# Two graph-transformer layers on one core: the 20-token tile moved to the last block of each layer and spread over four column tiles of the array

## The chip, the cores and the metric

One core of one Trainium2 chip. The time is device microseconds from the first to the last instruction's work of one execution; the number to predict is the median of the runs of the changed kernel. All matrices are float32.

## The reference, cut to what matters

There are 2708 tokens of 512 features and a sparse symmetric adjacency with the diagonal set (about 9 neighbours of a token, never more than 23 counted with itself). Each of two layers does:

```python
q, k, v = h @ Wq.T + bq, h @ Wk.T + bk, h @ Wv.T + bv      # 8 heads of 64
attn    = softmax(where(mask, q.k / 8, -1e9))               # over the neighbours
h1 = layer_norm(h + (attn @ v) @ Wo.T + bo)
h2 = layer_norm(h1 + relu(h1 @ W1.T + b1) @ W2.T + b2)      # 512 -> 2048 -> 512
```

The second layer takes the first one's `h2` as its `h`.

## The kernel before, in words

`by_edges` never builds the 2708 x 2708 scores. It first lists each token's neighbours, sorts the tokens by how many they have, and cuts the sorted order into 22 tiles, numbered 0 (most neighbours) to 21. 2708 is 21 times 128 plus 20, so tile 21 has only 20 tokens, and these have the fewest neighbours. `CAPS` gives the neighbour slots of each tile: 22 for tile 0, 6 for tile 19, 5 for tile 20, 3 for tile 21. (`by_rows` is a dense fallback behind a branch that these inputs do not take.)

Attention of a tile works slot by slot on VectorE (DVE), ScalarE (ACT) and GpSimd (POOL). For each slot POOL gathers one key-and-value row for every token (line 982). The slots go in chunks of up to two: DVE multiplies by the queries (line 1019) and sums by head (line 1025), ACT takes the exponential (line 1038), ACT and DVE scale the values (lines 1045 and 1051), and DVE adds them up (line 1058). When a tile's slots are through, DVE makes the sums and reciprocals (lines 1066 to 1081) and ACT writes the divided context `cx` (line 1089). A tile of 20 tokens costs as much per slot as one of 128, since the cost goes with the row length.

TensorE (PE) does the dense part. `project` (line 569) is four accumulating products, one per 128 features, with the tokens as the stationary operand and 512 weight columns moving: it makes k, v, q and the output projection o. `feed_forward` takes a block of two tiles side by side: in each of 16 steps f it makes a 128-feature slice of the hidden layer (`pf`, line 1312: the weights are stationary, the block's tokens move, so 148 or 256 columns), ACT applies relu (`ft`, line 1320), and three steps later (`LAG`) each of the block's two tiles gets its second product, 512 columns moving, into its own accumulator `a` (line 1300). Then DVE adds the residual (line 1332) and normalises (lines 1128 to 1138, with one power on POOL at line 1134).

Eleven blocks make a layer. Before, the order is (21, 20), (19, 18), (8, 9), (7, 10), (6, 11), (0, 17), (1, 16), (2, 15), (3, 14), (4, 13), (5, 12). Attention follows the same order and runs ahead of PE by credits: `advance` lets some chunks be issued per step, `through(k)` issues everything until block k's contexts exist. Late in block k (step 10 or 11) the contexts of block k+1 are transposed (`tp<-ident,cx`, line 1144), projected with Wo, normalised, and in the last step transposed again (`tp<-ident,h`) as the next block's input. Beside the next block's steps the first layer makes the second layer's k and v of the finished block (`keys_values`, lines 1362 to 1376).

The first block of a layer is special, since there is no block before it to hide its attention. In layer 0 it runs beside `first_queries` (22 projections, line 909 takes them out of PSUM); the first tiles' own queries are computed from gathered rows by `own_query` (line 955), so that their attention need not wait for the stored queries. In layer 1 it runs beside 16 of the layer's query projections (line 1242), and can start only when the last block's k and v are in memory.

The order on PE, ACT and the SP queue is written out by hand; DVE and POOL are ordered by a planner, except where they too are set by hand.

Of the kernel before, what the change touches and what calls it, by code (L numbers as in the profile page):

```python
# [19 lines left out]
DM = 512  # L20
# [11 lines left out]
SAFE = 60.0  # L32
LIST = 24
SEG = 247

CAPS = (22, 14, 13, 12, 12, 11, 11, 10, 10, 9, 9, 9, 9, 8, 8, 8, 7, 7, 7, 6, 5, 3)
SLOTS = 2
# [7 lines left out]
QT = 6  # L45
OWN = 13
EARLY = 3
FIRST = 4
PACE = (0.62, 0.72)


# [420 lines left out]
def by_edges(ctx: ExitStack, tc: tile.TileContext, x, xT, adj, layers, out, good):  # L472
# [92 lines left out]
    def project(xs, r, wm, name, other=False):  # L565

        o = (ps_f if other else ps).tile([P, DM], F32, tag="f" if other else "g", name=name)
        for c in range(NC):
            nc.tensor.matmul(o[:r], xs(c), wm[:, c, :], start=(c == 0), stop=(c == NC - 1))  # L569
        return o  # L570

    def finish(steps):
        for _ in steps:
# [7 lines left out]
    def size(g):  # L581
        return min(P, N - g * P)
# [231 lines left out]
    def first(w, meanwhile):  # L814

        xg = []

        def load():
            i = len(xg)
            b = i % XBS * XB  # L820
            bw = min(XB, N - b)
            t = wts.tile([P, NC, XB], F32, tag=f"w1_{5 + i % 3}", name="xg")
            xg.append(t)
            step = bw if i else P
            for a in range(0, bw, step):
# [24 lines left out]
        wv = matrix(w, "Wv", "wv")  # L850
        pa = tc.tile_pool(name="pa", bufs=2)
        lists, counted, ranked, listed = lists_of(pa.__enter__())
        done, before = 0, None
        for t in range(NT):
            r = size(t)
            xs = tokens(t, 0)
            kv = wts.tile([P, 2 * DM], F32, tag=f"w2_{5 + t % 3}", name="kvs")
            k = project(xs, r, wk, "k")
            if t == 0:
                finish(turning)  # L860
            nc.vector.tensor_tensor(kv[:r, :DM], k[:r], bk[:r], ALU.add)
            v = project(xs, r, wv, "v", other=True)
            nc.scalar.copy(kv[:r, DM:], v[:r])
            if before:
                nc.scalar.dma_start(**before)
            before = dict(out=kv_d[0][t * P : t * P + r, :], in_=kv[:r])
            if t == 0:
                finish(load())
            while done < min(NT, 1 + LEAD * t):
                lists(done)  # L870
                done += 1
                if done == NT:
                    counts = counted()
            meanwhile(t)
            if t == QT:
                wq = matrix(w, "Wq", "wq")
                turning = turned_row(cols[1], "bq", DK**-0.5)
                bq = next(turning)
                finish(turning)
        nc.scalar.dma_start(**before)  # L880
        return bq, wq, counts, ranked, listed, pa, tokens

    def first_queries(bq, wq, counts, ranked, listed, pa, tokens, meanwhile):
# [14 lines left out]
        for t in range(NT):  # L898
# [7 lines left out]
            if t % 2 == 0:  # L906
# [2 lines left out]
            nc.vector.scalar_tensor_tensor(  # L909
                qs[:r, t % 2], q[:r], DK**-0.5, bq[:r], ALU.mult, ALU.add  # L910
            )
            if t == OWN - 1:
# [38 lines left out]
    def own_query(g, zT, to, bq, wq):  # L951

        r = size(g)
        q = project(lambda c: zT[:, c, :r], r, wq, "q")
        nc.vector.scalar_tensor_tensor(to[:r], q[:r], DK**-0.5, bq[:r], ALU.mult, ALU.add)

    def checked():

# [194 lines left out]
    class Layer:  # L1153
# [83 lines left out]
        def query(self, g, zT):  # L1237

            r = size(g)
            q = project(lambda c: zT[:, c, :r], r, self.wq, "q")  # L1240
            qs = dn.tile([P, DM], F32, tag="row", name="qs", bufs=3)
            nc.vector.scalar_tensor_tensor(
                qs[:r], q[:r], DK**-0.5, self.bq[:r], ALU.mult, ALU.add
            )
            self.kept()
            self.due = (g, qs)

# [7 lines left out]
        def attended(self, block, got):  # L1255
# [11 lines left out]
            for g, r, cT, xb in cTs:  # L1267
                o = project(lambda c: cT[:, c, :r], r, self.wo, "o")
                h = dn.tile([P, DM], F32, tag="h", name="h", bufs=4)
                nc.vector.tensor_tensor(h[:r], o[:r], xb[:r], ALU.add)  # L1270
                if self.n == 0:
                    nc.vector.tensor_tensor(h[:r], h[:r], self.bo[:r], ALU.add)
                norm(h, r, self.g1, self.e1b2)
# [13 lines left out]
        def feed_forward(self, block, hs, hT):  # L1287
# [5 lines left out]
            def second(f, only=None):  # L1293
                c0 = 0
                for g, a in zip(block, accs):
                    r = size(g)
                    if only not in (None, g):
                        c0 += r
                        continue
                    nc.tensor.matmul(  # L1300
# [3 lines left out]
                        start=(f == 0),  # L1304
                        stop=(f == NFC - 1),
                    )
                    c0 += r

            for f in range(NFC):
# [11 lines left out]
                fts.append(ft)  # L1321
                if f >= LAG:
                    second(f - LAG)
                yield None
            for g in block:
                for f in range(NFC - LAG, NFC):
                    second(f, g)
            zs = []
            for g, a, h in zip(block, accs, hs):
                r = size(g)  # L1330
                z = h
                nc.vector.tensor_tensor(z[:r], a[:r], h[:r], ALU.add)  # L1332
                norm(z, r, self.g2, self.e2)
                if self.n == NL - 1:
                    nc.gpsimd.indirect_dma_start(
# [10 lines left out]
        def keys_values(self, block, zs):  # L1346
# [12 lines left out]
            for i, (g, z, zT) in enumerate(zip(block, zs, zTs)):  # L1359
                r = size(g)  # L1360
                kv = kvs[:, i, :]
                k = project(lambda c: zT[:, c, :r], r, self.kv[0], "k")
                nc.vector.tensor_tensor(kv[:r, :DM], k[:r], self.bk[:r], ALU.add)
                v = project(lambda c: zT[:, c, :r], r, self.kv[1], "v")
                nc.scalar.copy(kv[:r, DM:], v[:r])
                nc.sync.dma_start(out=zT_d[n][g], in_=zT)
                nc.sync.dma_start(out=xb_d[n][g * P : g * P + r, :], in_=z[:r])
                yield
# [293 lines left out]
```

## Time and profile before

| what | value |
|---|---|
| three runs, median (lowest to highest) | 1954.73 us (1953.54 to 1954.83) |
| the profiled execution, span | 1950.7 us |
| PE busy in it | 1892.6 us (97%) |
| DVE, ACT, POOL busy | 1300.1, 933.4, 797.9 us |
| mean granted TensorE clock | 0.992 |

The profiled span is 4.0 us below the median of the three runs. In the rows, a float32 product of TensorE is two records, each with its own load of the stationary operand; `128*20` behind an operation means 128 rows and 20 columns of the array in use, `128*128` all of it. A record's duration [...]overlaps the next one, so the pace of a row of products is read from start to start.

### The profile page before, as it was taken

The numbers are of one execution on the slowest core, as the hardware profiler recorded it, in microseconds if no ns is written. First come the engines' busy times: TensorE is split into PE (matmuls) and PEld (weight loads), VectorE is DVE, ScalarE is ACT, GpSimd is POOL, SyncE is SP. The second block draws the span as 40 slices with busy tenths as digits, with TensorE's granted clock in tenths as the row PEclk, the third lists the DMA queues.
The fourth block names the chain that finished last, engine by engine and source line by source line (L and its number), as shares of the span: only waits on it lengthen the run. The fifth ranks groups of instructions, "written<-read, shape, count | busy, mean of one in ns | idle before, by whom it ended". The sixth has DMA issues, their size and how long they took to land.

```text
span 1950.7 us, 20853 instructions
## 1 busy us (share of the span) xinstructions
PE 1892.6 (97%) x6162; PEld 1100.7 (56%) x6162; DVE 1300.1 (67%) x2142; ACT 933.4 (48%) x3219; POOL 797.9 (41%) x710
## 2 busy tenths in 40 slices
PE   9999988999999898999999999999999999999997
PEld 4444433565656555566565643556666666666664
DVE  5884576685957859577552116898597989877421
ACT  4660254464555655446441112665457765755410
POOL 3114535453644636445210004554255756554110
PEclk9999998999999999999999999999999999999999
DMA  9998766554745746455320548756465757563000
GB/s 330 355 307 296 265 211 219 177 193 137 235 153 173 235 146 231 146 177 190 110 90 22 194 152 315 253 207 207 137 236 169 253 188 265 184 202 127 11 11 13
DMA packets 131487, 366.92 MB, mean 188 GB/s; under 512 B 16669, under 2 KB 36989, under 8 KB 128655
## 3 DMA queue, kind: packets, MB, share of 16 engines
q0 software_dynamic: 69120, 246.35, 38.0%
q1 hardware_dynamic: 53332, 99.66, 14.9%
q10 hardware_dynamic: 8910, 19.48, 2.6%
q8 instruction: 50, 0.82, 0.2%
q14 instruction: 75, 0.61, 0.1%
HBM read 314.62 MB, written 50.83 MB: 187 GB/s over the span
## 4 chain that ended last, share of the span: by engine, by line
PE 54%; issue 3%; DVE 2%; POOL 1%; DMA 1%; ACT 1%; POOLq 0%; SPq 0%; DVEq 0%
PE a L1300 21%; PE pf L1312 21%; PE o L569 5%; PE q L569 2%; PE k L569 2%; PE v L569 2%; PE tp L1144 1%; POOL kv L982 1%; DVE kv L1019 0%; DVE sc L1025 0%; DMA zT<-zT_d 0%; DMA kv<-kv_d,idx 0%; ACT hT L1149 0%; ACT kv L1045 0%; DMA kv_d<-kvs,ident_i 0%
## 5 line engine op out<-in xcount | busy, mean ns | idle before, releaser
L982 POOL DMA_INDIRECT kv<-kv_d,idx x420 | 540.6, 1287 | 459.8 <-DVE acc L1058 265.3
L1300 PE MATMUL a<-w,ft 128*128 128x512 f32 (+1 forms) x1408 | 663.7, 597 | 3.2 <-ACT ft L1320 3.2
L1312 PE MATMUL pf<-hT,w 128*128 128x256 f32 (+1 forms) x2816 | 636.6, 373 | 14.5 <-ACT ft L1320 10.1
L1312 PEld LDWEIGHTS pf<-hT,w 128*128 128x128 f32 x2816 | 521.5, 191 | 192.3 <-issue 104.1
L1320 ACT ACTIVATE ft<-pf,b 128x256 f32<-128x256 f32 (+1 forms) x352 | 159.8, 460 | 481.8 <-PE pf L1312 473.1
L1300 PEld LDWEIGHTS a<-w,ft 128*128 128x128 f32 (+1 forms) x1408 | 255.7, 186 | 226.4 <-issue 202.5
L1019 DVE TENSOR_TENSOR kv<-kv,q 128x1024 f32<-128x1024 f32 (+3 forms) x222 | 254.4, 1157 | 178.5 <-DMA kv<-kv_d,idx 147.3
L1045 ACT ACTIVATE kv<-kv,p 128x64 f32<-128x64 f32 x1232 | 311.0, 335 | 5.0
L1025 DVE TENSOR_REDUCE sc<-kv 128x16 f32<-128x1024 f32 (+3 forms) x222 | 254.2, 1152 | 1.5
L1058 DVE TENSOR_TENSOR acc<-acc,kv 128x1024 f32<-128x1024 f32 (+2 forms) x178 | 203.8, 1145 | 22.4 <-ACT kv L1045 21.3
L1134 POOL TENSOR_TENSOR rd<-va,mhalf 128x1 f32<-128x1 f32 (+1 forms) x88 | 88.9, 1011 | 290.4 <-DVE va L1132 289.4
L569 PE MATMUL o<-wo,cT 128*128 128x512 f32 (+1 forms) x352 | 155.1, 593 | 0.5 <-ACT cT L1149 0.5
L1051 DVE TENSOR_TENSOR kv<-kv,p 128x512 f32<-128x512 f32 (+1 forms) x178 | 121.3, 683 | 45.7 <-ACT p L1038 45.7
L1038 ACT ACTIVATE p<-sc,minus 128x8 f32<-128x8 f32 (+1 forms) x420 | 102.9, 295 | 66.6 <-DVE sc L1025 48.4
L1089 ACT ACTIVATE cx<-acc,su 128x64 f32<-128x64 f32 (+1 forms) x352 | 88.5, 334 | 69.3 <-DVE su L1081 54.3
L569 PEld LDWEIGHTS o<-wo,cT 128*128 128x128 f32 (+1 forms) x352 | 65.1, 186 | 86.5 <-issue 75.2
L1332 DVE TENSOR_TENSOR h<-a,h 128x512 f32<-128x512 f32 (+1 forms) x44 | 29.8, 676 | 106.7 <-PE a L1300 106.7
L1138 DVE SCALAR_TENSOR_TENSOR h<-h,rd,ln_b 128x512 f32<-128x512 f32 (+1 forms) x88 | 65.7, 747 | 49.0 <-POOL rd L1134 49.0
L663 ACT ACTIVATE code<-aj 128x2708 bf16<-128x2708 int32 (+1 forms) x22 | 73.2, 3327 | 48.3 <-POOL aj L659 46.8
L666 DVE MAX8 tops<-code 128x8 f32<-128x247 f32 (+2 forms) x242 | 83.1, 401 | 18.4 <-ACT code L663 18.3
L1045 ACT ACTIVATE acc<-kv,p 128x64 f32<-128x64 f32 (+1 forms) x352 | 88.8, 334 | 1.4
L569 PE MATMUL k<-wk,xg 128*128 128x512 f32 (+1 forms) x176 | 82.0, 610 | 5.4 <-DMA wk<-in_Wk 4.9
(133 smaller groups left out, 1460.4 us busy)
## 6 DMA issues: line engine op xcount, KB each, us to landing
aj<-in_adj SPq DMA_DIRECT2D x21, 1354.0 KB
kv_d<-kvs ACTq DMA_DIRECT2D x21, 512.0 KB
w<-in_W SPq DMA_DIRECT2D x20, 512.0 KB
xg<-in_xT SPq DMA_DIRECT2D x19, 512.0 KB
kv<-kv_d,idx POOLq DMA_INDIRECT x420
w<-in_W ACTq DMA_DIRECT2D x12, 512.0 KB
q_d<-qs SPq DMA_DIRECT2D x22, 256.0 KB
zT_d<-zT SPq DMA_DIRECT2D x22, 256.0 KB
```

The costliest lines, as they stand in the source:

```text
L569: nc.tensor.matmul(o[:r], xs(c), wm[:, c, :], start=(c == 0), stop=(c == NC - 1))
L982: nc.gpsimd.indirect_dma_start(out=to, out_offset=None, in_=table[:, :], in_offset=bass.IndirectOffsetOnAxis(ap=s, axis=0), bounds_check=N ...
L1019: nc.vector.tensor_tensor(kv[:r, :c, :DM], kv[:r, :c, :DM], self.q[:r].unsqueeze(1).to_broadcast([r, c, DM]), ALU.mult,)
L1025: nc.vector.tensor_reduce(self.sc[:r, s0 : s0 + c, :], kv[:r, :c, :DM].rearrange("p s (h d) -> p s h d", d=DK), AX.X, ALU.add,)
L1038: nc.scalar.activation(p[:r, s, :], self.sc[:r, s, :], AF.Exp, bias=minus[:r, g, s : s + 1])
L1045: nc.scalar.activation(to[:, i, hd], kv[:r, i, DM + h * DK : DM + (h + 1) * DK], AF.Copy, scale=p[:r, s0 + i, h : h + 1],)
L1051: nc.vector.tensor_tensor(to[:, 0, :].rearrange("p (h d) -> p h d", d=DK), kv[:r, 0, DM:].rearrange("p (h d) -> p h d", d=DK), p[:r, s0, : ...
L1058: nc.vector.tensor_tensor(self.acc[:r, :c, :], self.acc[:r, :c, :], kv[:r, :c, DM:], ALU.add)
L1134: nc.gpsimd.tensor_tensor(rd[:r], va[:r], mhalf[:r], ALU.pow)
L1300: nc.tensor.matmul(a[:r], fts[f][:, c0 : c0 + r], self.w2[f // 2][:, f % 2, :], start=(f == 0), stop=(f == NFC - 1),)
L1312: nc.tensor.matmul(pf[:, :w], self.w1[f // 2][:, c, f % 2 * P : f % 2 * P + P], hT[:, c, :w], start=(c == 0), stop=(c == NC - 1),)
L1320: nc.scalar.activation(ft[:, :w], pf[:, :w], AF.Relu, bias=self.b1[:, f : f + 1])
```

## The change

Four things change.

1. The order of the blocks: (20, 19), (18, 17), (7, 9), (6, 10), (5, 11), (0, 16), (1, 15), (2, 14), (3, 13), (4, 12), (21, 8). The 20-token tile goes from the first block to the last. `FIRST` (how many of the last tiles' lists are read back first) goes from 4 to 5, and the tiles with an own query in layer 0 are 20, 19, 18, 17 in place of 21, 20, 19, 18.
2. `project` of a tile of at most 32 tokens: the four products no longer accumulate in PSUM partitions 0 to 19; each goes alone to its own group of 32 partitions (0, 32, 64, 96), that is to its own 32 columns of the array.
3. `plus_rest`: DVE adds the three further parts, one instruction of 20 x 512 each, wherever such a product is taken out: k, v, q, o and the second feed-forward product.
4. The second feed-forward products of the 20-token tile are issued four at a time (`quarters`, after steps 3, 7, 11 and in the closing products), each hidden slice to its own group of columns; before they were one per step between the other tile's.

```diff
+Q4 = 32
-FIRST = 4
+FIRST = 5
     def project(xs, r, wm, name, other=False):
         o = ...
+        if r <= Q4:
+            for c in range(NC):
+                nc.tensor.matmul(
+                    o[c * Q4 : c * Q4 + r], xs(c), wm[:, c, :], start=True, stop=True
+                )
+            return o
         for c in range(NC):
             nc.tensor.matmul(o[:r], xs(c), wm[:, c, :], start=(c == 0), stop=(c == NC - 1))
         return o
+    def rest(o, r):
+        return [o[q * Q4 : q * Q4 + r] for q in range(1, 4)] if r <= Q4 else []
+    def plus_rest(to, o, r, scale=None):
+        for part in rest(o, r):
+            if scale is None:
+                nc.vector.tensor_tensor(to, part, to, ALU.add)
+            else:
+                nc.vector.scalar_tensor_tensor(to, part, scale, to, ALU.mult, ALU.add)
...
+            plus_rest(kv[:r, :DM], k, r)      # and after every v, q, o and a
...
-                    if only not in (None, g):
+                    if only not in (None, g) or r <= Q4:
+            def quarters(f):
+                c0 = 0
+                for g, a in zip(block, accs):
+                    r = size(g)
+                    for i in range(f - 3, f + 1) if r <= Q4 else ():
+                        q = i % 4 * Q4
+                        nc.tensor.matmul(
+                            a[q : q + r],
+                            fts[i][:, c0 : c0 + r],
+                            self.w2[i // 2][:, i % 2, :],
+                            start=(i < 4),
+                            stop=(i >= NFC - 4),
+                        )
+                    c0 += r
                 if f >= LAG:
                     second(f - LAG)
+                if f % 4 == 3 and f < NFC - 1:
+                    quarters(f)
             for g in block:
                 for f in range(NFC - LAG, NFC):
                     second(f, g)
+                    if g == block[-1] and f == NFC - LAG:
+                        quarters(NFC - 1)
...
-    blocks = [(NT - 1, NT - 2), (NT - 3, NT - 4)] + [
-        (i, NT - 5 - i) for i in (*range(8, 5, -1), *range(6))
-    ]
+    blocks = [(20, 19), (18, 17), (7, 9), (6, 10), (5, 11), (0, 16)]
+    blocks += [(1, 15), (2, 14), (3, 13), (4, 12), (NT - 1, 8)]
```

More of the change, by code (lines that the diff above doesn't have):

```diff
@@ L861, in first @@
             nc.vector.tensor_tensor(kv[:r, :DM], k[:r], bk[:r], ALU.add)
+            plus_rest(kv[:r, :DM], k, r)
             v = project(xs, r, wv, "v", other=True)
             nc.scalar.copy(kv[:r, DM:], v[:r])
+            plus_rest(kv[:r, DM:], v, r)
             if before:
@@ L911, in first_queries @@
             )
+            plus_rest(qs[:r, t % 2], q, r, DK**-0.5)
             if t == OWN - 1:
@@ L955, in own_query @@
         nc.vector.scalar_tensor_tensor(to[:r], q[:r], DK**-0.5, bq[:r], ALU.mult, ALU.add)
+        plus_rest(to[:r], q, r, DK**-0.5)
     def checked():
@@ L1244, in query @@
             )
+            plus_rest(qs[:r], q, r, DK**-0.5)
             self.kept()
@@ L1270, in attended @@
                 nc.vector.tensor_tensor(h[:r], o[:r], xb[:r], ALU.add)
+                plus_rest(h[:r], o, r)
                 if self.n == 0:
@@ L1332, in feed_forward @@
                 nc.vector.tensor_tensor(z[:r], a[:r], h[:r], ALU.add)
+                plus_rest(z[:r], a, r)
                 norm(z, r, self.g2, self.e2)
@@ L1363, in keys_values @@
                 nc.vector.tensor_tensor(kv[:r, :DM], k[:r], self.bk[:r], ALU.add)
+                plus_rest(kv[:r, :DM], k, r)
                 v = project(lambda c: zT[:, c, :r], r, self.kv[1], "v")
                 nc.scalar.copy(kv[:r, DM:], v[:r])
+                plus_rest(kv[:r, DM:], v, r)
                 nc.sync.dma_start(out=zT_d[n][g], in_=zT)
```

## The prediction

> **What bounds the kernel now.** I read the page first, then the groups by shape, then the time line of PE around the 20-token tile, last what ends PE's idle time.
>
> ```profile
> PE 1892.6 (97%) x6162; PEld 1100.7 (56%) x6162; DVE 1300.1 (67%) x2142; ACT 933.4 (48%) x3219; POOL 797.9 (41%) x710
> L1300 PE MATMUL a<-w,ft 128*128 128x512 f32 (+1 forms) x1408 | 663.7, 597 | 3.2 <-ACT ft L1320 3.2
> ```
>
> PE is the bound nearly everywhere: time taken off PE is gained, and any new idle time of PE is lost. The groups by shape give the work of the 20-token tile:
>
> ```profile
> L1300 PE MATMUL a<-w,ft 128*20 128x512 f32 x64 | 35.4, 649 | 0.0
> L569 PE MATMUL o<-wo,cT 128*20 128x512 f32 x16 | 7.2, 593 | 0.0
> L1300 PEld LDWEIGHTS a<-w,ft 128*20 128x20 f32 x64 | 4.4, 102 | 8.7 <-issue 7.7 <-ACT hT L1149 1.0
> ```
>
> The reader is to see that 20 tokens cost per record what 128 do, and that products are counted in pairs of records: 64 for 16 steps and two layers. The time line of PE, first block of layer 0:
>
> ```profile
> 166.79 44.80 PE L569 MATMUL q<-wq,xg 128*128 128x512 f32 x104
> 246.06 3.60 PE L569 MATMUL q<-wq,xg 128*128 128x512 f32 x8
> 249.59 7.24 PE L569 MATMUL o<-wo,cT 128*20 128x512 f32 x16
> 256.76 3.61 PE L569 MATMUL q<-wq,xg 128*20 128x512 f32 x8
> 260.30 3.70 PE L569 MATMUL q<-wq,zT 128*128 128x512 f32 x8
> 263.93 1.16 PE L1144 MATMUL tp<-ident,h 20*128 20x20 f32 x8
> 277.72 1.27 PE L1312 MATMUL pf<-hT,w 128*128 128x148 f32 x8 [2.81 <-ACT ft L1320]
> 293.30 2.06 PE L1312 MATMUL pf<-hT,w 128*128 128x148 f32 x8 [4.64 <-ACT ft L1320]
> 331.49 1.11 PE L1144 MATMUL tp<-ident,h 128*128 128x128 f32 x4 [2.72 <-DVE h L1138]
> 336.01 1.11 PE L1144 MATMUL tp<-ident,h 128*128 128x128 f32 x4 [3.40 <-DVE h L1138]
> ```
>
> Three readings. (a) The pace is 0.429 us per record (44.80 less a tail of 0.16, over 104). (b) Changing between full and narrow columns costs: the 16 records from 249.59 to 256.76 (8 narrow, 8 full) take 7.17 us where 16 x 0.429 is 6.86, so an excursion to narrow and back costs 0.31. (c) The first block waits for attention: 2.81 and 4.64, with 1.32 and 1.34 between them, then 2.72 and 3.40. Such gaps also slow the clock: in these two stretches it is the third number from the end (0.95, 0.63):
>
> ```profile
> 265.00:300.00 35.00, 24.43 (x100) 13.10 (x100) 29.77 (x39) 22.61 (x92) 16.85 (x13) 0.95 0.76 250
> 331.00:345.00 14.00, 10.10 (x23) 3.83 (x23) 8.19 (x15) 2.29 (x8) 9.68 (x8) 0.63 0.54 182
> ```
>
> **The change part by part, PE's work.** The tile has 68 products before: 32 second products, 8 of o, and 28 of k, v, q. Four of these (its own query) become a 128-token tile's at the same price. The other 64 become 16 sets of four on four column groups. A set costs 8 x 0.429 = 3.43 us before.
>
> What a set costs after is shown nowhere in this trace: all its narrow products use one column group. From below: the Trainium skill, "TensorEngine Tiling (Array Packing)", Theoretical Speedup, says that tokens of at most 32 may go up to four times as fast, since different tiles run in parallel; that makes a set 2 records long, 0.86, say 0.95 with issue. From above: no overlap, 3.43; and if each record's 0.100 us weight load (102 ns row) shows too, 4.2. A second rule speaks against the first: "TensorE: Matmul & The Clock Gate", Part 3, says that products start and end strictly in program order. The trace has two records per product, on the same columns, so the second must wait for the first, and the next product may only start with that second one. The order is then a, then b with the next a, and so on: 5 record times for 8 records, 5 x 0.429 = 2.15 us. I take 2.15. By the first rule the 16 sets save 16 x 2.48 = 39.7 us; by the second 16 x 1.28 = **20.5 us**.
>
> Excursions: before 14 per layer in the feed-forward (steps 0 to 12 one each, the last three together), and 7 in all for k and v (twice, adjacent), q (own, stored, layer 1) and o (twice): 35. After: 4 per layer and 6 for the others, 14. 21 x 0.31 = **6.5 us** saved, whatever the sets do.
>
> The hidden slices (148 columns against 256) move from the first to the last block, sum unchanged.
>
> **DVE's additions.** Ten places x 3 additions of 20 x 512, at 0.68 us (the 20-row `h<-o,xb` beside 255.67 took 0.67): 20 us on an engine that is 67% busy. They are hidden behind PE, with three exceptions. After the lists, k and v of tile 21 put 6 of them (3.7 us at 0.62 start to start) ahead of the ranks on DVE, which had 3.83 us idle just there waiting for PE: the ranks come at the same time. But then the 2.6 us that PE saves on k and v in layer 0 is given back where PE waits for gathered rows (0.48 us idle at 213.01 before): **+2.6**. Uncovered, these additions would add up to 3.7 more. At layer 0's end tile 21 and tile 8 are both normalised behind two queries (7 us of PE), 2 us more than before: covered. At the very end, in the order built from the changed kernel, one of the additions and tile 21's normalisation stand between tile 8's: **+1.5**.
>
> **The first block of each layer.** Its two tiles have 5 + 6 = 11 slots where they had 3 + 5 = 8, and the next block 14 in place of 13. Nothing stands before them to hide that.
>
> ```profile
> 243.41 2.02 ACT L1089 ACTIVATE cx<-acc,su 128x64 f32<-128x64 f32 x8 [4.08 <-DVE su L1078]
> 1207.83 2.02 ACT L1089 ACTIVATE cx<-acc,su 128x64 f32<-128x64 f32 x8 [9.48 <-DVE su L1081]
> 1212.25 1.01 PE L1144 MATMUL tp<-ident,cx 20*128 20x20 f32 x8
> ```
>
> Layer 0: the second context is done at 245.4 and PE takes it at once. DVE works without a gap up to it, so extra work there is late. In the changed DVE order, 14 slots of scores stand ahead of it (three of the next pair's) and 11 weighed, in place of 8 and 8: three more chunks of 1.21 + 1.22, one more weighed of 0.68 + 1.22, about 10 us in all. PE waits some 10 us at `tp<-ident,cx`; behind it are the last queries, o, and the whole block, and DVE's own h waits for that o. What comes back: the wide first block has 11.3 us more of its own work (128 records of 148 against 256 columns, 0.125 against 0.213) and 4.3 less of excursions, so attention that had it stalled for 16 us is covered better, the more as 3 slots are done already. Before, PE lost 16.7 us there in gaps and 35 x 0.05 + 14 x 0.37 = 6.9 to the clock, 23.6. After, I put 10 for the new wait, 2.5 for the clock behind it, 13.5 for what remains of the old gaps and their clock, and the 2.6 above, 28.6: **+5** (between -7, the old gaps gone and the new wait half hidden, and +15, all of them as before).
>
> Layer 1: the second context is ready at 1209.9, PE arrives at 1212.3, so 2.4 of slack. The changed order has 18 slots of scores and 11 weighed ahead of it, in place of 14 and 8, and three more queries to take out: 4.8 + 2.4 + 1.8 = 9. PE waits about 6 at its transposes, and the clock is slow after it for some 2: **+8** (0 if DVE's 4.37 us wait for a stored query at 1193.03 is absorbed and PE's own idle of 4.1 us there goes too; 13 if both stay).
>
> The SP queue has the same transfers; the last block has 17 us less of steps for the second layer's weights, but these are wanted some 60 us later: nothing.
>
> **Sum.** -20.5 - 6.5 + 5 + 8 + 1.5 = -12.5 on the span of 1950.7, 1938.2; with the 4.0 us by which the median lies above it, **1942 us**.
>
> **Rivals.**
> 1. The column groups run all four at once (a set near 0.95): -39.7 - 6.5 + 14.5 + 2.3 more given back at 213 = -29.4, 1925. For it: the skill's up to four times. Against: the paired records. Chance 0.20.
> 2. Something between, a set of about 2.8, the load of the next column group showing or only the halves of neighbours touching: -10 - 6.5 + 14 = -2.5, 1952. Chance 0.12.
> 3. The other side: the groups run one after another, so only the excursions are saved, and the longer first attention decides: -6.5 + 12 = +5.4, 1960. If each load shows too, 13 us more, 1973. The point from which it decides is a set of 2.9 us: 16 x (3.43 - 2.93) + 6.5 = 14.5. For it: no record here shows two products at once. Against: loads do run under products of other records here. Chance 0.18.
>
> **How the numbers follow.** The forecast, in-order pairs, has 0.50; its own range, from the ends of +5 and +8, is 1927 to 1955. It is faster by more than 0.2% (3.9 us, about what a measurement can tell) in 0.85 of it, rival 1 nearly always, rival 2 in 0.45, rival 3 in a tenth: 0.43 + 0.19 + 0.05 + 0.02 = 0.69. Within: 0.04 + 0.03 + 0.02 = 0.09. Slower 0.22. The range, from most of rival 1 to rival 3 without the loads, is 1920 to 1963.
>
> **What would show it.** Sets: narrow products of different quarters starting within some 0.01 us of the one before's second record, a set 2.15 long; all eight in 0.95 would be rival 1, 0.429 between all starts rival 3. First blocks: idle of PE before `tp<-ident,cx` near 250 of about 10 and near 1205 of about 6, waiting for ACT cx, and shorter gaps before the first block's `pf`. Excursions: 14. The prediction is wrong if the sets lie outside 1.8 to 2.6, or if attention of the first pair is not late.

## The result, and the profile after

The changed kernel takes 1943.05 us (median of 4 runs, 1941.27 to 1946.15); the kernel before, beside it, 1954.78. The ratio is 0.9944, with a 95% interval of 0.993 to 0.9958: 0.56% faster. Forecast were 1942 us and a range of 1920 to 1963. The number came out; the sum behind it did not. TensorE gained twice what was put down on the narrow products, and other terms took the surplus back.

The first lines of the page after (span, busy time of each engine), then the groups by shape of the narrow tile's products:

```profile
span 1944.3 us, 20898 instructions
PE 1858.4 (96%) x6162; PEld 1096.7 (56%) x6162; DVE 1321.0 (68%) x2172; ACT 934.7 (48%) x3219; POOL 809.3 (42%) x710
```
```profile
L1339 PE MATMUL a<-w,ft 128*20 128x512 f32 x64 | 8.4, 600 | 0.0
L571 PE MATMUL o<-wo,cT 128*20 128x512 f32 x16 | 2.1, 599 | 0.0
```

The second products of the narrow tile were 64 records in 35.4 us and are 64 in 8.4; `o` went from 7.2 to 2.1. PE's busy time fell by 34.2 us, the span of the profiled execution by 6.4 (this execution was the slowest of the four, 1946.15). So PE stands idle longer, as the share of 96% for 97% says too.

How a set runs is read from PE's time line (start, duration, operation, records, and in brackets the idle time before it and what ended it):

```profile
154.22 1.06 PE L571 MATMUL k<-wk,xg 128*20 128x512 f32 x8
155.09 1.04 PE L571 MATMUL v<-wv,xg 128*20 128x512 f32 x8
162.20 6.43 PE L576 MATMUL q<-wq,xg 128*128 128x512 f32 x8 [6.07 <-DVE kvs L879]
...
263.15 1.91 PE L1166 MATMUL tp<-ident,cx 128*128 128x128 f32 x4 [14.21 <-ACT cx L1111]
...
285.24 1.11 PE L1166 MATMUL tp<-ident,h 128*128 128x128 f32 x4 [3.66 <-DVE h L1160]
...
1093.60 1.05 PE L1339 MATMUL a<-w,ft 128*20 128x512 f32 x8
...
1211.87 1.91 PE L1166 MATMUL tp<-ident,cx 128*128 128x128 f32 x4 [7.43 <-ACT cx L1111]
```

From the set of k at 154.22 to that of v at 155.09 it is 0.87 us for eight records, two record times of 0.43; before it was eight, 3.43. The single records in the trace say the same: the first records of k's four products start at 154.218, 154.225, 154.232 and 154.238, the second ones from 154.662 on. All four column groups run at once.

Three waits are new or much longer. After k and v of the 20-token tile the first query waits 6.07 us for DVE. The second context of the first pair makes PE wait 14.21 us in layer 0 and 7.43 in layer 1. Before, PE took that context at once in layer 0, and in layer 1 it was ready 2.4 us ahead of PE.

What the first query waits for is seen in DVE's time line after:

```profile
161.46 1.87 DVE L879 TENSOR_TENSOR kvs<-k,bk 128x512 f32<-128x512 f32 x3
163.36 1.40 DVE L586 TENSOR_TENSOR kvs<-k,kvs 20x512 f32<-20x512 f32 x2
169.56 0.43 DVE L777 TENSOR_TENSOR hot<-hot,pr 128x264 f32<-128x264 f32 x1 [1.92 <-PE pr L770]
```

It is line 879, which takes k out of PSUM and stands on DVE behind the work on the lists; before, it came at nearly the same time (160.40), and PE was still busy with k and v. The additions (line 586) come behind it.

For the contexts, in layer 0 the window from 250 to 290 (columns: length, busy time and instructions of PE, PEld, DVE, ACT, POOL, granted clock, DMA share, GB/s), first of the kernel before:

```profile
250.00:290.00 40.00, 33.99 (x124) 15.47 (x122) 34.52 (x46) 20.14 (x82) 15.71 (x12) 1.00 0.61 206
```
```profile
250.00:290.00 40.00, 22.66 (x60) 10.83 (x61) 25.46 (x39) 9.39 (x37) 7.71 (x7) 0.75 0.35 114
```

The second line is the kernel after: PE works 22.66 us of 40, and at a clock of 0.75. The first slice of feed-forward starts at 286.8 for 265.5. This is 21.3 us behind, though the kernel is faster at the end. By stages of the two profiled executions (start of the stage, before and after, in us):

| stage | before | after | difference |
|---|---|---|---|
| up to the first `pf` of layer 0 | 265.5 | 286.8 | +21.3 |
| from there to the first `pf` of its last block | 807.5 | 801.8 | -5.7 |
| from there to the first `pf` of layer 1 | 156.3 | 144.3 | -12.0 |
| from there to the first `pf` of its last block | 653.4 | 658.0 | +4.6 |
| from there to PE's last instruction (`pr<-held,ones`) | 55.2 | 34.7 | -20.5 |
| from there to the end | 12.8 | 18.7 | +5.9 |

The narrow block moved from the first row to the last ones, so a row is not the gain of its stage alone; the sum is -6.4.

The last row was hardly in the forecast. The end of the kernel before, then after, in the time line of POOL and of the last DVE steps:

```profile
1942.02 0.75 DVE L1138 SCALAR_TENSOR_TENSOR h<-h,rd,ln_b 128x512 f32<-128x512 f32 x1 [0.47 <-POOL rd L1134]
1943.06 1.03 POOL L1335 DMA_INDIRECT out<-h,ident_i  x1 [1.08 <-DVE h L1138]
```
```profile
1930.90 1.40 DVE L1160 SCALAR_TENSOR_TENSOR h<-h,rd,ln_b 20x512 f32<-20x512 f32 x2 [0.47 <-POOL rd L1156]
1931.96 1.16 POOL L1379 DMA_INDIRECT out<-h,ident_i  x1 [0.57 <-DVE h L1160]
1936.58 1.01 POOL L1379 DMA_INDIRECT out<-h,ident_i  x1 [3.47 <-issue]
```

Before, the last write of the output goes 0.3 us after its rows are ready. After, both tiles are ready at 1932.3, the first write goes, and the second goes at 1936.58. In the trace POOL's queue stands 4.07 us in a semaphore wait of line 1379 between them, until the first write has landed: both write the tensor `out` by an index, and the program lets the second wait for the first one's semaphore. Before, the two tiles were 3.6 us apart, and the wait of that queue (1.13 us there) ended before the second tile was ready.

A write by an index need not hold back the next one. The 22 writes of the lists to their ranks also go into one tensor by an index:

```profile
171.85 1.10 POOL L789 DMA_INDIRECT rec_d<-rec,ranks  x1 [20.29 <-DVE ranks L785]
173.25 1.00 POOL L789 DMA_INDIRECT rec_d<-rec,ranks  x1 [0.30 <-issue]
```

They start at most 1.6 us apart, and none lands in less than 2.1 us from its issue (median 4.6), so each is issued before the one ahead of it has landed. The kernel declares these writes independent (`tc.declare_no_dep(..., reason="no two tokens have one rank")`, line 797); the two writes of the output have no such line.

### The profile page after: what moved, and what is told of

Read it like the earlier page. It is cut to its first block, busy times and chain, and to the rows that moved or that the text cites. A ratio compares the mean times of both kernels' runs of the same rounds, so it can differ in the third digit from the quotient of the medians.

```text
span 1944.3 us, 20898 instructions
## 1 busy us (share of the span) xinstructions
PE 1858.4 (96%) x6162; PEld 1096.7 (56%) x6162; DVE 1321.0 (68%) x2172; ACT 934.7 (48%) x3219; POOL 809.3 (42%) x710
## 5 line engine op out<-in xcount | busy, mean ns | idle before, releaser
L1004 POOL DMA_INDIRECT kv<-kv_d,idx x420 | 547.0, 1302 | 452.2 <-DVE acc L1080 273.5
L1324 PE MATMUL a<-w,ft 128*128 128x512 f32 x1344 | 632.2, 596 | 5.3 <-ACT ft L1359 4.4
L1324 PEld LDWEIGHTS a<-w,ft 128*128 128x128 f32 x1344 | 253.2, 191 | 198.6 <-issue 171.6
L1080 DVE TENSOR_TENSOR acc<-acc,kv 128x1024 f32<-128x1024 f32 (+2 forms) x178 | 204.0, 1146 | 18.9 <-ACT kv L1067 17.0
L576 PE MATMUL o<-wo,cT 128*128 128x512 f32 x336 | 151.1, 602 | 0.5 <-ACT cT L1171 0.5
L1060 ACT ACTIVATE p<-sc,minus 128x8 f32<-128x8 f32 x420 | 102.8, 294 | 69.2 <-DVE sc L1047 62.1
L576 PEld LDWEIGHTS o<-wo,cT 128*128 128x128 f32 x336 | 64.5, 193 | 83.2 <-issue 72.9
L1160 DVE SCALAR_TENSOR_TENSOR h<-h,rd,ln_b 128x512 f32<-128x512 f32 (+1 forms) x88 | 65.6, 747 | 40.6 <-POOL rd L1156 40.6
L1410 ACT COPY kvs<-v 128x512 f32<-128x512 f32 (+1 forms) x22 | 12.9, 586 | 158.9 <-PE v L576 138.5
```

The source lines that it names most:

```text
L1004: nc.gpsimd.indirect_dma_start(out=to, out_offset=None, in_=table[:, :], in_offset=bass.IndirectOffsetOnAxis(ap=s, axis=0), bounds_check=N ...
L1060: nc.scalar.activation(p[:r, s, :], self.sc[:r, s, :], AF.Exp, bias=minus[:r, g, s : s + 1])
L1080: nc.vector.tensor_tensor(self.acc[:r, :c, :], self.acc[:r, :c, :], kv[:r, :c, DM:], ALU.add)
L1324: nc.tensor.matmul(a[:r], fts[f][:, c0 : c0 + r], self.w2[f // 2][:, f % 2, :], start=(f == 0), stop=(f == NFC - 1),)
```

## The experiments

Ratios are to the kernel before, run on the same chip beside them; its median lay at 1956 to 1958 us in these runs, so kernels are compared by ratio where they come from different groups of runs. The changed kernel's own is 0.9944 [0.993, 0.9958].

**1. New order and sets, but one column group.** The narrow products accumulate in one group again, with no additions.

```diff
     def project(...):
-        if r <= Q4:
-            for c in range(NC):
-                nc.tensor.matmul(o[c * Q4 : c * Q4 + r], ..., start=True, stop=True)
-            return o
     def rest(o, r):
-        return [o[q * Q4 : q * Q4 + r] for q in range(1, 4)] if r <= Q4 else []
+        return []
             def quarters(f):
-                a[q : q + r], ..., start=(i < 4), stop=(i >= NFC - 4)
+                a[:r], ..., start=(i == 0), stop=(i == NFC - 1)
```

> The changed kernel with the 20-token products back on one column group, accumulating as before, in the same places and in the same groups of four; the additions of the parts fall away. Theory A (four column groups run at once and save 2.54 us per set, and the later first attention takes much of it back): PE busy about 40 us more than in the changed kernel; of the 16 sets the two of layer 0's k and v gained nothing, and the ranks come 3.4 us earlier without the additions, so about 32 us more than the changed kernel's 1943, near 1975, that is some 20 slower than before. The wait for the second context near 250 stays, at about 10. Theory B (the additions on VectorE cause the new waits): near 1955, since the waits go with them. Theory C (only the fewer changes of array width paid): same as the changed kernel, 1943.

Measured: 1968.44 us, ratio 1.0076 [1.0054, 1.0098]. The column groups are worth 1.3%, some 26 us, in the new order; without them the change makes the kernel slower. PE's time line of this kernel:

```profile
259.19 1.91 PE L1160 MATMUL tp<-ident,cx 128*128 128x128 f32 x4 [14.19 <-ACT cx L1105]
```

The 14 us wait is there to 0.02 us. It comes from the new order of blocks, not from the additions. The 6.07 us wait is not: 0.57 at that place, so that one comes with the column groups. This run takes away the faster k and v and the additions together; the time line above, where the query waits for line 879 ahead of all additions, says that it is the faster k and v.

**2. Column groups in the old order.**

```diff
-FIRST = 5
+FIRST = 4
-    blocks = [(20, 19), (18, 17), (7, 9), (6, 10), (5, 11), (0, 16)]
-    blocks += [(1, 15), (2, 14), (3, 13), (4, 12), (NT - 1, 8)]
+    blocks = [(NT - 1, NT - 2), (NT - 3, NT - 4)] + [
+        (i, NT - 5 - i) for i in (*range(8, 5, -1), *range(6))
+    ]
```

> The column groups, the sets of four and the additions kept, but the order of the blocks as before (tile 21 with tile 20 in the first block). Theory A: the price of the order goes away, about 25 us of idle and slow clock at the two starts, but the savings on the tile (o, own query, second products) now lie in a first block that waits for attention, so less than half of them counts there: 1930, between 1920 and 1943. The first context wait near 250 is under 4 us. Theory B (the additions cause the waits): the same waits as in the changed kernel, 1943 or more.

Measured: 1954.12 us, ratio 0.9994 [0.9979, 1.0008]: no difference from before. PE's busy time is 1866.1, 26.5 less than before, and as much came back as idle time between its records (40.6 us before, 68.2 here). The time line of this kernel shows where:

```profile
280.80 1.90 PE L1339 MATMUL a<-w,ft 128*20 128x512 f32 x2 [5.62 <-ACT ft L1359]
285.41 1.89 PE L1339 MATMUL a<-w,ft 128*20 128x512 f32 x2 [2.71 <-ACT ft L1359]
302.02 2.16 PE L1339 MATMUL a<-w,ft 128*20 128x512 f32 x4 [5.23 <-ACT ft L1359]
...
1269.30 1.90 PE L1339 MATMUL a<-w,ft 128*20 128x512 f32 x2 [4.11 <-ACT ft L1359]
```

A set asks for the relu slice of the step just issued, where a product of the wide tile asks for the one three steps back. In the first block ACT is busy with attention and its relu is late. In the last block, where the new order has the sets, it is not (0.0 idle in the group above). So two parts of the change that look independent are not: the sets need the move to the last block, or a later place in the step (7 below).

**3. Layer 0's keys and values of the 20-token tile not split.** Their six additions fall away.

```diff
-        if r <= Q4:
+        if r <= Q4 and split:            # split=False for k and v of layer 0
...
```

> The changed kernel with layer 0's k and v of the 20-token tile whole, accumulating on one column group, without their six additions. Theory A: PE waited 6.07 us right behind them for VectorE, so the 5.1 us of products come in that gap at no cost, and the ranks come 3.4 us earlier; that and everything behind them up to the first contexts moves by 3.4: 1940. Theory B (that wait and the ranks do not matter, since the first contexts wait for a gather): 1943, no change.

Measured: 1943.59 us (1936.36 to 1946.58), ratio 0.9935 [0.9911, 0.9959], not to be told from the changed kernel. The wait at the first query is gone and its 5.1 us are spent in PE's work:

```profile
154.22 3.61 PE L576 MATMUL k<-wk,xg 128*20 128x512 f32 x8
157.66 3.60 PE L576 MATMUL v<-wv,xg 128*20 128x512 f32 x8
161.71 3.70 PE L576 MATMUL q<-wq,xg 128*128 128x512 f32 x8 [0.45 <-DVE kvs L879]
```

With the groups the first query starts at 162.20, without them at 161.71. So at this place the column groups gain nothing at all: what PE saves on k and v, it waits for DVE. They even cost: behind the wait the query takes 6.43 us for 3.70, so it ends 3.2 us later than here. The granted clock of that stretch, first of the changed kernel, then of this one (columns as in the windows above):

```profile
162.00:170.00 8.00, 7.80 (x15) 4.03 (x16) 5.87 (x10) 0.57 (x1) 0.00 (x0) 0.64 0.82 275
162.00:170.00 8.00, 8.00 (x23) 4.19 (x23) 2.73 (x7) 0.57 (x1) 1.09 (x1) 1.00 0.96 315
```

In the profiled executions layer 0's second block starts at 359.9 here for 365.2, and the span is 2.9 us shorter; the medians do not show a gain.

**4. Two groups of columns.** The projections' four products go to groups 0, 0, 1, 1, the second products of a set to 0, 1, 0, 1; two of each accumulate.

```diff
-                    o[c * Q4 : c * Q4 + r], ..., start=True, stop=True
+                    o[c // 2 * Q4 : c // 2 * Q4 + r], ..., start=(c % 2 == 0), stop=(c % 2 == 1)
...
-                        q = i % 4 * Q4
+                        q = i % 2 * Q4
...
```

> The changed kernel with two column groups in place of four. The projections are issued as group 0, 0, 1, 1, the second products as 0, 1, 0, 1. If products start strictly in program order, a projection's second pair starts only with the last record of the first pair: 7 record times, 3.0 us a set. If each group takes its own next record as soon as it is free, 4 record times, 1.72. The second products take 1.72 either way, and the two halves of a product show as in the changed kernel, all first halves together and then all second ones. The time is 10 to 15 us above the changed kernel's.

Measured, in one run: 1950.17 us. PE's time line:

```profile
153.94 1.91 PE L571 MATMUL k<-wk,xg 128*20 128x512 f32 x8
155.67 1.90 PE L571 MATMUL v<-wv,xg 128*20 128x512 f32 x8
...
1089.08 1.90 PE L1340 MATMUL a<-w,ft 128*20 128x512 f32 x8
```

Both kinds take four record times (1.73 us from k to v). In the projection's order, the third product is the first of group 1. Its first record starts 13 ns after the first product's (153.935 and 153.948), long before the second product of group 0 can. (A record does not name its group; but with one group the records start 0.43 us apart, so two that start 13 ns apart are on different groups.) A product therefore does not wait for the start of the one before it in the program if that one stands in another column group's line: each group takes its own next record. This is the experiment that ends the forecast's reading of the order. The time is 7 us above the changed kernel's median where 10 to 15 were expected; one run does not say more.

**5. Tile 18's own query two queries later (layer 0).** Before the second context DVE has work for the next pair. In the changed kernel it stands there, in DVE's time line and then ACT's:

```profile
253.19 1.23 DVE L1041 TENSOR_TENSOR kv<-kv,q 128x1024 f32<-128x1024 f32 x1 [4.63 <-DMA kv<-kv_d,idx]
...
260.22 0.69 DVE L1041 TENSOR_TENSOR kv<-kv,q 128x512 f32<-128x512 f32 x1 [1.21 <-DMA kv<-kv_d,idx]
...
261.55 0.23 DVE L1100 TENSOR_REDUCE su<-p 128x8 f32<-128x48 f32 x1
```
```profile
262.51 2.02 ACT L1111 ACTIVATE cx<-acc,su 128x64 f32<-128x64 f32 x8 [11.98 <-DVE su L1103]
```

Those two multiplications are tile 18's, put ahead of tile 19's last sums by the planner, and their rows have not arrived. Everything of tile 19 is queued behind them. They need tile 18's own query, so issuing that later moves them:

```diff
             if t == OWN + 4:
-                own_query(order[2], zTs[2], to[order[2]], bq, wq)
                 zT = turned_own(order[3], xr)
+            if t == NT - 3:
+                own_query(order[2], zTs[2], to[order[2]], bq, wq)
```

> From the changed kernel; layer 0's own query of tile 18 is issued two queries later, so that the two multiplications of tile 18 that stood ahead of tile 19's last sums on VectorE now stand behind them. Theory A (of the 14.21 us that the first transposes of cx wait, about half is VectorE standing before tile 18's gather, 4.63 and 1.21 us, with 19's sums queued behind it): the wait falls to 7 to 9 us, the first pf comes at 279 to 282 instead of 286.8, and the total falls by 3 to 7 us, to 1936 to 1940. Theory B (the wait falls, but tile 18 is late by as much for block 1, and the gain is given back there): wait 7 to 9 us, new waits of 4 us or more before 380, total 1941 to 1946. Theory C (19's own gathers set cx): the wait stays at 12 us or more and the total at 1941 to 1946.

Measured: 1935.87 us, ratio 0.99 [0.9885, 0.9915]. PE's and ACT's time lines of this kernel:

```profile
255.26 1.90 PE L1167 MATMUL tp<-ident,cx 128*128 128x128 f32 x4 [4.79 <-ACT cx L1112]
```
```profile
254.62 2.02 ACT L1112 ACTIVATE cx<-acc,su 128x64 f32<-128x64 f32 x8 [3.17 <-DVE su L1104]
```

The context is ready 7.9 us earlier, the wait falls from 14.21 to 4.79 (part of it because the query itself now lies in front of it), the first `pf` starts at 279.8 for 286.8, and these 7 us reach the end. About half of the wait was DVE standing before a transfer (4.63 and 1.21 us) for work that nobody needed yet.

**6. Both early repairs together** (3 and 5).

> The same delay of tile 18's query, and in layer 0 the keys and values of tile 21 by the wide form without additions (only those 8 products are not split). Theory A (both early delays, the 6.07 us before the first query and VectorE's stand before 18's gather, reach the end): first pf at 275 to 279, total 1933 to 1938. Theory B (layer 0's gathers and VectorE give it back by block 1 or 2, as they did when only the keys and values were left whole): first pf the same, waits of 6 us or more in sum between 300 and 400, total 1941 to 1945.

Measured: 1931.66 us, ratio 0.988 [0.9864, 0.9896]. First `pf` at 274.9. This is the fastest kernel with nothing left out or displaced: 1.2% below the kernel before, more than twice the gain of the change as it was made. Its interval touches that of 5 alone, so the share of 3 in it is not settled.

**7. The old order with the sets one step later.** A set is issued after the next step's `pf` and the wide tile's product, ahead of that step's relu.

```diff
+                if f % 4 == 0 and f:
+                    second(f - LAG)
+                    quarters(f - 1)
                 ft = dn.tile([P, 2 * P], F32, tag="ft", name="ft", bufs=4)
...
-                if f >= LAG:
+                if f >= LAG and f % 4:
                     second(f - LAG)
-                if f % 4 == 3 and f < NFC - 1:
-                    quarters(f)
...
```

> The old order of blocks with the column groups, where each set of four second products of the narrow tile is issued one step later: after the next slice's pf and the wide tile's product, ahead of that slice's relu. Theory A (the old order lost its saving because the sets ask for the relu slice just issued, waits of 5.62, 2.71, 5.23 us in layer 0 and 4.11 and smaller ones in layer 1): those waits fall to 3 us or less each, and the total falls from 1954 to 1942 to 1949. Theory B (ScalarE and VectorE are the bound while the first block runs, so the wait only moves to the next product): the sum of waits between 262 and 345 stays within 4 us of 25.7, and the total is 1951 to 1956.

Measured: 1941.9 us, ratio 0.9928 [0.9914, 0.9943]. As a total this is the first theory, and it is as fast as the changed kernel without its move of blocks. By layers it is not so plain. In layer 1 the waits before sets (9.4 us in five places) shrink to one of 3.83, and the first block takes 56.7 us from its first `pf` to that of the next block, where it took 69.2 in experiment 2 and 63.4 before. In layer 0 the waits from the first `tp<-ident,h` to 345 do not shrink (28.6 us in experiment 2, 30.5 now), and that block does not gain: the wait only moves (before the last two `tp<-ident,h`, which wait for DVE, 7.6 us became 11.3). The windows of experiment 2, then of this kernel, over the first block of layer 0 and over that of layer 1 from its first `pf` to the next block's:

```profile
262.00:345.00 83.00, 58.14 (x231) 33.60 (x232) 64.14 (x91) 39.30 (x154) 43.71 (x35) 0.78 0.66 223
1222.90:1292.10 69.20, 59.79 (x241) 32.24 (x242) 60.27 (x79) 43.42 (x172) 36.66 (x27) 0.93 0.73 243
```
```profile
262.00:345.00 83.00, 55.17 (x228) 32.56 (x228) 63.95 (x91) 39.80 (x157) 41.17 (x33) 0.79 0.65 217
1229.50:1286.20 56.70, 52.87 (x240) 31.56 (x241) 51.68 (x69) 43.14 (x172) 32.20 (x26) 0.97 0.82 286
```

In layer 1 the same 240 records take 12.5 us less: 5.6 less idle, and 6.9 less busy. The clock is 0.97 for 0.93, and fewer sets are broken up by a wait for a slice; how much each of the two makes was not separated. In layer 0 nothing changes, at a clock of 0.78 and 0.79.

**8. The same, with layer 0's keys and values of the tile not split.**

> The last kernel with layer 0's keys and values of tile 21 by the wide form without additions. Theory A (the 5.11 us that the first query waits in the old order for VectorE are on the path): 4 to 6 us faster than the late sets alone. Theory B (given back before block 0 by tile 20's gathers): within 2 us of it.

Measured: 1940.63 us, ratio 0.9919 [0.9906, 0.9932], within the interval of 7. In the two profiled executions layer 0's second block starts 4.4 us earlier (343.6 for 348.0), and the span is 3.5 us shorter; the medians are 1.3 us apart. So the 4 to 6 us are there in the time line, and the totals do not confirm them.

**9. Idle waits filled with products that nobody reads.** Behind the waits the granted clock is low. If the wait is what lowers it, work in its place should help.

```diff
+    def fill(m):
+        pr = ps_f.tile([P, DM], F32, tag="f", name="fl")
+        for _ in range(m):
+            nc.tensor.matmul(pr, now.wo[:, 0, :P], now.wo[:, 1, :], start=True, stop=True)
...
             through(0)
+            fill(12)                     # layer 1: fill(7)
             early[0] = now.attended(blocks[0], got)
```

> The changed kernel with twelve products of 128x512 that nobody reads, 10.3 us in all, issued on TensorE just before layer 0's first transposes of cx (where it waits 14.21 us), and seven, 6.0 us, before layer 1's (where it waits 7.43 us). Theory A (a wait of TensorE costs more than its length: the granted clock, 0.66 and 0.84 in the 40 us from 250, falls because of the wait): the waits shrink to 3 to 5 and 1 to 3 us, the clock in these rows returns to 0.95 or more, and the total falls by 3 to 7 us, to 1936 to 1940. Theory B (the clock falls for another reason, or the slow records lie beside other waits): clock or total unchanged, 1941 to 1946. If the fill is not covered by the wait, the total rises.

Measured: 1944.09 us, ratio 0.9927 [0.9912, 0.9943]: no measurable difference from the changed kernel. The waits shrank as meant, 14.21 to 5.30 and 7.43 to 2.77. The window from 250 to 290 of this kernel:

```profile
250.00:290.00 40.00, 32.29 (x83) 13.73 (x81) 23.99 (x36) 11.64 (x46) 10.30 (x10) 0.91 0.44 141
```

The clock in it is 0.91 for 0.75, and in the 60 us after it 0.91 where the changed kernel has 0.97. So the slow stretch moved behind the next waits rather than going away. A wait's price in clock could not be bought back in this way.

**10. The same in the fastest kernel,** with four and seven products.

> The fastest kernel so far (tile 18's own query issued later, layer 0's keys and values of tile 21 whole) with four such products, 3.4 us, before layer 0's first transposes of cx, where 4.80 us of wait are left, and seven, 6.0 us, before layer 1's, where 7.40 us are left. Theory A: 2 to 5 us faster than without them, 1926 to 1930. Theory B: within 2 us of 1931.7.

Measured: 1932.55 us, ratio 0.9888 [0.9868, 0.9908]; the kernel without them has 0.988. Nothing gained.

**11. Plain writes at the very end.** The last block's two outputs go by direct transfers on ACT's and SP's queues. The rows then land in the order of the sorted tiles and not at their tokens' places, so the output is wrong: those 148 tokens' own rows are left out and other tokens' rows are overwritten. The number and size of the rows written are the same.

```diff
-                if self.n == NL - 1:
+                if self.n == NL - 1 and block == blocks[-1]:
+                    by = nc.scalar if g == block[0] else nc.sync
+                    by.dma_start(out=out[g * P : g * P + r, :], in_=z[:r])
+                elif self.n == NL - 1:
                     nc.gpsimd.indirect_dma_start(out=out, ...)
```

> The changed kernel, with the outputs of the very last block written by plain transfers on ScalarE's and SP's queues in place of POOL's two indirect ones. In the changed kernel both tiles are ready at about 1932.3 us, but POOL's queue holds the second write for 4.07 us until the first has landed. Theory A (that wait is on the path, and the predicted tail of 1.5 is 5.9 because of it): the span after the last product of TensorE falls from 18.7 us by 3.5 to 6, and the total by as much, to 1937 to 1940. Theory B (the end is set by something else, such as the check that closes the program or how late a plain transfer lands): total within 2 us of 1943.

Measured: 1937.88 us, ratio 0.9903 [0.9883, 0.9922]. Its time line at the end:

```profile
1918.36 0.19 PE L1650 MATMUL pr<-held,ones 128*1 128x1 f32 x2
...
1924.44 0.33 ACTq L1380 DMA_DIRECT2D out<-h  x1
1925.10 0.34 SPq L1380 DMA_DIRECT2D out<-h  x1
```

The second write follows the first by 0.66 us. From PE's last instruction to the end (a span of 1931.9) it is 13.5 us for 18.7: 5.2 us, as the theory of the serial writes has it. In the changed kernel POOL stands idle for 3.47 us between its two writes; the other 1.7 may be the other kind of transfer. A kernel with the two indirect writes declared independent, which would tell that apart and keep the output right, was not run.

**12. The same in the fastest kernel.**

> The fastest kernel so far (tile 18's own query later, layer 0's keys and values of tile 21 whole) with the same plain writes at the end. Theory A: 3.5 to 6 us faster than without them, 1926 to 1929. Theory B: within 2 us of 1931.7.

Measured: 1926.15 us, ratio 0.9833 [0.9815, 0.9851]. The tail is 13.4 us for 18.9. It has the same misplaced rows, so it shows what is there to gain and is no kernel to keep.

## Why the prediction was right, and where it was wrong

The sum against the two profiled executions (idle time is PE's between records; the forecast's +5 and +8 include some slow clock, which on the measured side falls under "rest"; "rest" is what is missing to -6.4 and was not measured by itself):

| term | predicted | measured |
|---|---|---|
| sixteen sets | -20.5 | 16 x (3.43 - 0.87) = -41.0 |
| excursions, 35 to 14 | -6.5 | 14 counted, -6.5 at 0.31 each (0.32 around a set in the trace after) |
| layer 0 up to its second block | +5 | idle 17.7 to 33.1: +15.4 |
| layer 1 up to its second block | +8 | idle 5.1 to 14.2: +9.1 |
| idle elsewhere | 0 | -2.4 |
| the tail | +1.5 | 12.8 to 18.7: +5.9 |
| rest | - | +13.1 |
| sum | -12.5 | -6.4 |

By its own sign, "wrong if the sets lie outside 1.8 to 2.6", the prediction is wrong: the sets take 0.87. That the time was met is luck.

**The set.** The failed step is "5 record times for 8 records", taken from the rule of the Trainium skill, "TensorE: Matmul & The Clock Gate", Part 3, that products start and end strictly in program order. The runs show 2 record times with four groups and 4 with two, in both orders of issue. The other rule that was weighed, up to four times by "TensorEngine Tiling (Array Packing)", Theoretical Speedup, is the one that the trace bears out: 3.43 over 0.87 is 3.9. The forecast had it as rival 1, at a chance of 0.20. Its objection, that a product is two records on the same columns, only means that the two records of one group follow each other; the four groups do so side by side.

**Layer 0's start.** Right in kind: PE does wait at `tp<-ident,cx`, and DVE is late. It was put at about 10 us and is 14.21, and two steps failed. "About 10 us in all" counted the instructions that DVE has ahead of the context and not that two of them wait for rows: 4.63 and 1.21 us in the trace, and experiment 5 takes most of that back. And "the ranks come at the same time" failed: their first record moved from 168.40 to 171.85. The additions did fit into most of DVE's 3.83 us of idle time, for they end at 167.64 and DVE then waits 1.92 us more for PE (`pr`, above). Late was PE: its query, which those products stand behind, starts 0.72 us later and takes 6.43 us for 3.70, together the 3.45. What the step left out is that k and v's 6.9 us had covered the time until DVE comes to line 879: the gain on k and v was put down as given back at the gathered rows (0.28 us of idle there), and it was given back at once, with a slow clock on top. The later gaps of the first block did shrink as forecast (16.2 to 8.3 us).

**Layer 1's start.** A wait of 6 us was forecast at the second context and is 7.43; +8 stands beside +9.1. Experiment 1 has 7.61 at that place without column groups, so it belongs to the order.

**The tail.** The added instructions are nearly as forecast: from PE's last instruction to the last rows 6.7 us for 4.8, 1.9 more where 1.5 were put. What the step left out is who waits for whom on POOL's queue: the change brings the two tiles' ends together, and so a wait into the open that had always been there. The forecast looked at DVE alone there and not at the queue of the output writes.

**The rest.** 13 us lie in slower records. The mean granted clock went from 0.992 to 0.981, and its low rows lie at and behind the waits (0.75 in the window above). At one place the runs tie it to a wait: from 162 to 170 us the clock is 0.64 behind the 6.07 us wait and 1.00 in experiment 3, where the wait is gone; experiments 5 and 6 (0.59 and 1.00) and 7 and 8 (0.78 and 1.00) say the same. The products ahead of the wait change along with it in these pairs, so even there the wait is not alone. For the whole rest it is argued, not shown. Experiment 7 speaks for it (5.6 us less idle, 6.9 less in the records of the same block), experiment 9 against: filling the waits moved the slow stretch and left the time.

**The rivals.** The forecast's own range, 1927 to 1955, is narrower than the ends of its +5 and +8 give together, 1922 to 1957. Rival 1 had the mechanism, and its 1925 missed the time because its waits were the forecast's, too small. Rivals 2 and 3 fall with the set, though the "longer first attention" of rival 3 is real: experiment 1 is that case, 1968 where it said 1960. So the forecast's time was met by errors of opposite sign that happened to cancel: 20.5 us too little gained on the sets; against it, 10 too little lost at layer 0's start, 4 at the end, and a rest of 13 not foreseen. (By medians the gain is 11.7 us, not the 6.4 of the profiled execution, which was a long one.)

## What to carry to other kernels

When work on the bounding engine becomes cheaper, ask first what that work was covering: here the narrow products hid DVE's late work on k, late relus and the first contexts, and 41 us less work became 12 us of time, and 23 once two early waits were dealt with. An instruction that stands first on an engine and waits for rows nobody needs yet costs as much as the work queued behind it, so look at what a planner may put ahead of the chain that the bound engine waits for. At the end of a kernel, look for a write that waits until another has landed: where two writes by an index never meet, declare it, as this kernel does for its ranks (for the output this was not run).

## What the runs showed that was not expected

Products on different column groups of TensorE overlap fully: four groups start within 21 ns, eight float32 records take 0.87 us, and with groups in the order 0, 0, 1, 1 group 1 starts 13 ns after group 0, ahead of a product that comes earlier in the program. Two writes of the output by an index follow each other on POOL's queue only when the first has landed, a wait of 4.07 us at the end, while 22 such writes that are declared independent go at most 1.6 us apart. Filling 10.3 and 6.0 us of TensorE's idle time with unread products raised the granted clock at that place from 0.75 to 0.91 and lowered it from 0.97 to 0.91 in the 60 us behind; the total did not change.
